# Two heads of a graph attention layer transposed by VectorE squares and SBUF transfers instead of TensorE

## The chip, the cores and the metric

The kernel runs on one core of a Trainium2 chip. The metric is the device time of one execution in microseconds. Before the change it is 3526.25 us, the median of three runs (3525.72 to 3527.4).

A core has five engines, each with its own queue of instructions in a fixed order: TensorE (PE; its weight loads are listed as PEld), VectorE (DVE), ScalarE (ACT), GpSimd (POOL) and SyncE (SP). All transfers of this kernel are issued from SP's queue; 16 DMA engines carry them out. TensorE reads SBUF and writes PSUM, which has eight banks here; VectorE or ScalarE brings a result from PSUM to SBUF (an eviction).

## The reference

`x` is 32 graphs of 512 nodes with 256 channels, in float32; `adj` is one 512 x 512 matrix for all. Four graph layers follow each other, each with its input added and a layer norm:

```python
x = _layernorm(x + _L0_gnn_ref(x, adj, ...))   # a: attention, 1 head
x = _layernorm(x + _L1_gnn_ref(x, adj, ...))   # b: transformer block, 8 heads of 32
x = _layernorm(x + _L2_gnn_ref(x, adj, ...))   # c: attention, 4 heads of 64
x = _layernorm(x + _L3_gnn_ref(x, adj, ...))   # d: bilinear attention
```

The third layer is the one whose transposes change:

```python
q = (h @ W).reshape(B, N, H, D)                       # H = 4 heads, D = 64
e = e_src[:, :, None, :] + e_dst[:, None, :, :]       # from two vectors a_src, a_dst
e = jnp.where(e >= 0, e, ALPHA * e)
e = jnp.where(mask, e, NEG_INF)
attn = jax.nn.softmax(e, axis=2)
h_prime = jnp.einsum('bijh,bjhd->bihd', attn, q)      # then elu
```

In each layer and head a graph has a 512 x 512 matrix of weights, exponentiated by rows. TensorE sums over the partitions, so to multiply this matrix with the values it has to be turned first. That is done square by square (128 x 128).

## The kernel before, in words

A graph's 512 nodes are four row blocks of 128 (`NB` = 4), handled in two halves (`F` = 2) of two blocks. A score tile `t` is one row block of one head, 128 x 512, in SBUF.

For a head of the first or third layer (class `Gat`), `attend` does this: TensorE spreads the row of destination scores over all partitions (`dst`, L755); VectorE adds the mask and takes the row maxima (`masked`, L637); ScalarE makes the bias, applies the leaky slope (L666) and the exponential with row sums (L672), in `leaky_softmax`; TensorE turns the four squares of each tile (`turn`, L549) into a PSUM bank; ScalarE or VectorE evicts that into `pT` (L492 or L494, in `copied`); and TensorE multiplies with the values (`weighted`, L561, for the third layer, two heads together; `rows_weighted`, L807, for the first and fourth). The third layer does heads 0 and 1, then heads 2 and 3. The second layer's scores are L853, its reduction L867, its exponentials L874; the fourth layer's scores are L975.

`finish` of each layer adds the input on POOL (`added`, L629), takes statistics on VectorE with a power on POOL (L603 to L609) and normalises (`normed`, L617) into the next layer's `x`. The last layer normalises into one more `x` tile, and SP stores that (L1041). SP also loads `xT` and `x` of each graph (`load`, L340); both are asked for ahead of the graph's first product.

The order of the work is not written by hand. Every step is an `op` with the engines that may do it and a duration in us that the kernel's author wrote beside it, what it reads and writes, and which pool's buffers it takes (`BUFS`: 18 tiles `t`, 8 halves `pT`, 6 `x`, and so on). `Plan.order` plays these steps through when the kernel is built: whenever an engine is free in this play, it takes the ready step with the best key. The key is made of the graph's number times `AGE`, the length of the work behind the step, and `URGENT` for the engine and stage (a letter for the layer, and 0 to 4 for projection, scores, finish, transposes, weighted product). On TensorE, `SWITCH_WEIGHT` adds a price for changing between full-array, row-tiled and column-tiled products. Up to four graphs (`WINDOW`) are in work at once. The result is one fixed order for each engine and one fixed choice of buffers and of the evicting engine; on the chip each engine goes through its order and waits where data or a buffer is not ready.

Of the kernel before, what the change touches and what calls it, by code (L numbers as in the profile page):

```python
# [14 lines left out]
ALU = mybir.AluOpType  # L15
# [12 lines left out]
BUFS = dict(t=18, pT=8, x=6, xT=3, v=5, qk=4, y=5, e=2, n=2, nT=2, hT=2, oT=4, small=8)  # L28
# [11 lines left out]
AGE = {"PE": 51, "ACT": 138, "DVE": -107, "POOL": 461, "SP": 20}  # L40
URGENT = {
    "PE": {"a0": -417, "a1": 491, "a2": -867, "b0": -448, "b1": 197, "b2": 839, "c0": -557, "c1": -258, "c2": 203, "d0": -909, "d1": -511, "d2": -1186, "a3": 1287, "a4": 1218, "b3": -47, "b4": 169, "c3": 2234, "c4": 712},
    "ACT": {"a0": -671, "a1": 422, "a2": 770, "b0": 459, "b1": 253, "b2": 93, "c0": 729, "c1": 136, "c2": -360, "d0": 573, "d1": -523, "d2": -1234, "a3": 806, "a4": -162, "b3": 370, "b4": 340, "c3": 698, "c4": -390},
    "DVE": {"a0": -247, "a1": 1195, "a2": 496, "b0": 1368, "b1": 273, "b2": -132, "c0": -1160, "c1": 19, "c2": 666, "d0": -845, "d1": -1056, "d2": -1458, "a3": 1297, "a4": 438, "b3": -527, "b4": 175, "c3": 138, "c4": 1482},
    "POOL": {"a0": -896, "a1": -817, "a2": 582, "b0": 3, "b1": -713, "b2": 227, "c0": -148, "c1": -607, "c2": 1624, "d0": 582, "d1": 1022, "d2": -1512, "a3": -446, "a4": 431, "b3": 270, "b4": 1342, "c3": 708, "c4": 734},
    "SP": {},
# [6 lines left out]
SWITCH_WEIGHT = 661  # L53
# [45 lines left out]
class Plan:  # L99
# [7 lines left out]
    def op(self, where, issue, writes=(), reads=(), takes=(), lag=0.0, port=False, form="full"):  # L107
# [10 lines left out]
        for buf in takes:  # L118
            if not buf.users and buf.tag is not None:
                o.takes.append(buf)  # L120
                self.bufs.append(buf)
                buf.users.append(o)
# [15 lines left out]
        o.after.discard(o)  # L138

# [153 lines left out]
def gnn_stack(  # L293
# [43 lines left out]
    def load(dst, out_ap, in_ap, cell=None, kb=256):  # L337
        def issue(e):
            with nc.allow_non_contiguous_dma(reason="vectors of 256 values by channel"):
                nc.sync.dma_start(out=out_ap(), in_=in_ap)  # L340

        op({SP: 0.1 + kb * 0.003}, issue, [dst if cell is None else (dst, cell)], [], lag=2.0)
# [136 lines left out]


# [62 lines left out]
    def turn(t, pT, i, name):  # L543

        ps = bank([P, NB, P], name)

        def issue(e):
            for j in range(NB):
                nc.tensor.transpose(ps[:, j], t[:, block(j)], ident)  # L549

        op({PE: 0.44}, issue, [ps], [t], [pT])
        copied(N, lambda: pT[:, :, block(i)], lambda: ps[:], [(pT, i)], [ps])

    def weighted(pv, oT, pTs, v, lo, D, us):

        def issue(e):
            for j in range(NB):
                for h, pT in enumerate(pTs):  # L560
                    nc.tensor.matmul(  # L561
                        pv[h * D : (h + 1) * D], lhsT=v[:, j, lo + h * D : lo + (h + 1) * D],
                        rhs=pT[:, j], start=(j == 0), stop=(j == NB - 1), skip_group_check=True,
                    )

        op({PE: us}, issue, [pv], [v] + pTs, [oT], form="columns")
# [13 lines left out]
    def scaled(dst, cell, lo, ps, inv, D):  # L580


        def issue(e):
# [5 lines left out]
                inv[:].unsqueeze(3).to_broadcast([P, FB, n // D, D]),  # L589
# [22 lines left out]
    def normed(y, dst, cell, lo, name):  # L612
# [8 lines left out]
        op({DVE: 0.66}, issue, [(dst, cell)], [y, mv, rstd], port=True)  # L621
# [11 lines left out]
    def masked(s, t, top, at, i):  # L633


        def issue(e):
            nc.vector.tensor_tensor_reduce(  # L637
                out=t[:], in0=s[:], in1=neg[:, i], scale=1.0, scalar=LOWEST, op0=ALU.add,
                op1=ALU.max, accum_out=top[(slice(None),) + at],
            )  # L640

        op({DVE: 0.61}, issue, [t, top], [s, (neg, i)])

    def leaky_softmax(ts, top, v, src, H, f, name):
# [3 lines left out]
        bias = tiny("bias", [P, FB, H], f"{name}_bias")  # L648
        total = tiny("total", [P, FB, H], f"{name}_total")
        inv = tiny("inv", [P, FB, H], f"{name}_inv")  # L650
        if src is not None:
            op(
                {DVE: 0.1},
                lambda e: nc.vector.tensor_tensor(top[:], top[:], v[:, part(f), src : src + H], ALU.add),
                [top], [(v, 2 * f), (v, 2 * f + 1)],
            )

        def negated(e):
            nc.scalar.activation(bias[:], top[:], AF.Prelu, alpha=SLOPE)
            nc.scalar.mul(bias[:], bias[:], -1.0)  # L660

        op({ACT: 0.3}, negated, [bias], [top])
        for (h, i), t in ts.items():

            def leaky(e, h=h, i=i, t=t):
                nc.scalar.activation(  # L666
                    t[:], t[:], AF.Prelu, alpha=SLOPE,
                    bias=0.0 if src is None else v[:, f * FB + i, src + h : src + h + 1],
                )

            def exp(e, h=h, i=i, t=t):
                nc.scalar.activation(  # L672
                    t[:], t[:], AF.Exp, bias=bias[:, i, h : h + 1], accum_out=total[:, i, h : h + 1]
                )

            op({ACT: 0.53 if src is None else 0.62}, leaky, [t], [] if src is None else [(v, f * FB + i)])
            op({ACT: 0.71}, exp, [t, total], [bias])
        pTs = []
        for h in range(H):
            pT = buf("pT", [P, NB, FN], f"{name}_pT{h}", FB)  # L680
            for i in range(FB):
                turn(ts[h, i], pT, i, f"{name}_tr{h}{i}")
            pTs.append(pT)
        op({DVE: 0.1}, lambda e: nc.vector.reciprocal(inv[:], total[:]), [inv], [total])
        return pTs, inv
# [30 lines left out]
    class Gat(Layer):  # L716
# [5 lines left out]

        def prepare(self, f):
# [17 lines left out]
        def attend(self):  # L741
            H, D, name, v = self.H, C // self.H, self.name, self.v
            G = min(H, P // D) if H > 1 else 1
            for g in range(0, H, G):
                ts = {}
                for h in range(G):
                    dst = bank([P, N], f"{name}_dst{g}{h}")
                    for i in range(NB):
                        ts[h, i] = buf("t", [P, N], f"{name}_t{g}{h}{i}")
# [7 lines left out]
                    op({PE: 0.44}, issue, [dst], [v], [ts[h, i] for i in range(NB)])  # L757
                    if h == 0:
                        tops = [
                            tiny("top", [P, FB, G], f"{name}_top{g}{f}") for f in range(F)  # L760
                        ]
                    for i in range(NB):
                        masked(dst, ts[h, i], tops[i // FB], (i % FB, slice(h, h + 1)), i)
                for f in range(F):
                    plan.stage = name[0] + "3"
                    pTs, inv = leaky_softmax(
                        {(h, i): ts[h, f * FB + i] for h in range(G) for i in range(FB)},
                        tops[f], v, C + g, G, f, f"{name}_{g}_{f}",
                    )
                    y = self.part_y(f)  # L770
                    plan.stage = name[0] + "4"
                    if H > 1:
                        pv = bank([P, FN], f"{name}_pv{g}{f}")
                        oT = buf("oT", [P, 1, FN], f"{name}_oT{g}{f}")
                        weighted(pv, oT, pTs, v, g * D, D, 1.86)
                        copied(FN, lambda oT=oT: oT[:, 0], lambda pv=pv: pv[:], [oT], [pv])
                        ps = turned_back(oT, 1, y, f"{name}_{g}{f}")
                        op({DVE: 0.4}, scaled(y, 0, g * D, ps, inv, D), [y], [ps, inv])
                    else:
                        pv = bank([P, FB, C], f"{name}_pv{f}")  # L780
                        rows_weighted(pv, pTs[0], v, y)
                        op({DVE: 0.62}, scaled(y, 0, 0, pv, inv, C), [y], [pv, inv])
# [18 lines left out]
    def rows_weighted(pv, pT, v, y):  # L801

        for i in range(FB):

            def issue(e, i=i):
                for j in range(NB):
                    nc.tensor.matmul(  # L807
                        pv[:, i], lhsT=pT[:, j, block(i)], rhs=v[:, j, 0:C],
# [3 lines left out]
            op({PE: 1.73}, issue, [pv], [(pT, i), v], [y])  # L812

    class Transformer(Layer):
# [14 lines left out]
        def attend(self):  # L829
            name, q_sb, k_sb = self.name, self.q, self.k  # L830
            for f in range(F):
# [4 lines left out]
                for c in range(NC):  # L836
                    ts = {}
                    for i in range(FB):
                        all_s = {}
                        for q0 in range(0, Q, S_HEADS):  # L840
                            heads = range(q0, q0 + S_HEADS)
                            ss = {
                                q: bank([P, N], f"{name}_s{f}{c}{i}{q}") for q in heads
                            }
                            for q in heads:
                                ts[q, i] = buf("t", [P, N], f"{name}_t{f}{i}{c}{q}")

                            all_s.update(ss)

                            def scores(e, i=i, ss=ss, c=c, f=f):  # L850
                                for q, s in ss.items():
                                    at = slice(q * D1, (q + 1) * D1)
                                    nc.tensor.matmul(  # L853
                                        s[:], lhsT=q_sb[at, c, block(f * FB + i)], rhs=k_sb[at, c],
                                        start=True, stop=True,
                                    )

                            op(
                                {PE: 0.95}, scores, list(ss.values()), [(q_sb, f), k_sb],
                                [ts[q, i] for q in heads], form="rows",  # L860
# [233 lines left out]
```

## Time and profile before

| | |
|---|---|
| median of three runs | 3526.25 us |
| profiled execution | 3525.66 us |
| its span, first to last instruction | 3523.9 us |
| granted TensorE clock | 0.999 |
| TensorE busy | 3501.5 us (99%) |
| VectorE busy | 2973.8 us (84%) |
| ScalarE busy | 2807.6 us (80%) |
| GpSimd busy | 869.1 us (25%) |
| transfers' share of the 16 DMA engines | 4.9% |
| transposes of score tiles (L549) | 7168 squares |
| SP queue waiting for the last layer's rows (L1041) | 3349.8 us |

A group line of the profile reads: line, engine, operation, written tile <- read tiles, shape, count | busy us, mean ns of one | idle us of the engine just before, and who ended it. A group's busy time is the union of its intervals; matmuls are pipelined, so one instruction's interval (274 ns) overlaps the next, and the tail of a group overlaps the group behind it. A timeline line has start, duration, engine, line, instruction and how many of them in a row. The chain of work that ended last is followed back from the last instruction to what released each step. Issue lines give count, size and the median time from issue to landing.

### The profile page before, as it was taken

To read this page: it belongs to the slowest core of one execution; us is meant where nothing else is said; L and a number is where in the kernel's file an instruction comes from. 1 tells how busy PE (TensorE), PEld (TensorE's weight loads), DVE (VectorE), ACT (ScalarE), POOL (GpSimd) and SP (SyncE) were. 2 spreads that over 40 slices of the span, in tenths; PEclk is the share of its full clock that TensorE was granted. 3 is DMA by queue.
4 is the path that set the end of the run, shared out by engine and by line. 5 is a ranking of instruction groups with operands and counts; after the bars stand their busy time and mean duration, and the time that the engine had idled before them with its cause. 6 is when DMAs were issued, how large, how long until landed. Compare 5 with 4: busy or idle time off the path is not lost.

```text
span 3523.9 us, 68878 instructions
## 1 busy us (share of the span) xinstructions
PE 3501.5 (99%) x24728; PEld 2685.4 (76%) x24728; DVE 2973.8 (84%) x8792; ACT 2807.6 (80%) x6856; POOL 869.1 (25%) x840
## 2 busy tenths in 40 slices
PE   8999999999999999999999999999999999999999
PEld 7777777778777787877878778687787877878777
DVE  7789888888888888888888888888888888888886
ACT  6798877878788787887888878887788877888786
POOL 1222222222222222222222222222222222222322
PEclk9999999999999999999999999999999999999999
DMA  3000100001000010000100001000010000100000
GB/s 95 7 2 1 37 1 19 19 1 37 1 19 19 1 37 1 19 19 1 37 1 19 19 1 37 1 19 19 1 37 1 19 19 1 37 1 19 19 7 19
DMA packets 56918, 59.41 MB, mean 17 GB/s; under 512 B 3968, under 2 KB 55808, under 8 KB 56576
## 3 DMA queue, kind: packets, MB, share of 16 engines
q1 hardware_dynamic: 56576, 55.00, 4.9%
q8 instruction: 196, 3.21, 0.4%
q14 instruction: 146, 1.20, 0.1%
HBM read 38.21 MB, written 16.78 MB: 16 GB/s over the span
## 4 chain that ended last, share of the span: by engine, by line
PE 99%; DVE 1%; ACT 0%; DMA 0%; issue 0%; SPq 0%; POOLq 0%; POOL 0%; DVEq 0%
PE ps L549 23%; PE ps L561 13%; PE ps L520 13%; PE ps L807 12%; PE ps L535 10%; PE ps L853 8%; PE ps L733 7%; PE ps L975 6%; PE ps L505 3%; PE ps L755 2%; PE ps L575 2%; DMA xT<-in_x_T 0%; SPq L340 0%; DVE st L603 0%; DVE rstd L606 0%
## 5 line engine op out<-in xcount | busy, mean ns | idle before, releaser
L549 PEld LDWEIGHTS ps<-ident,t 128*128 128x128 f32 x7168 | 805.5, 141 | 178.4 <-issue 38.7
L549 PE MATMUL ps<-ident,t 128*128 128x128 f32 x7168 | 898.4, 274 | 1.0 <-ACT t L874 0.8
L874 ACT ACTIVATE t<-t,low 128x512 f32<-128x512 f32 x1024 | 734.8, 735 | 41.5 <-DVE low L867 41.5
L492 ACT COPY pT<-ps 128x512 f32<-128x512 f32 x1099 | 594.1, 593 | 119.9 <-PE ps L549 116.4
L867 DVE CUSTOM_DVE_ANT_0 t<-ps,neg 128x512 f32<-128x512 f32 x1024 | 649.0, 686 | 46.2 <-PE ps L853 43.6
L629 POOL TENSOR_TENSOR y<-y,x 128x512 f32<-128x512 f32 x256 | 330.0, 1290 | 1371.7 <-DVE y L586 493.3
L609 POOL TENSOR_TENSOR rstd<-rstd,mhalf 128x2 f32<-128x2 f32 x384 | 297.2, 774 | 1049.1 <-DVE rstd L606 934.3
L637 DVE CUSTOM_DVE_ANT_0 t<-ps,neg 128x512 f32<-128x512 f32 x768 | 492.3, 683 | 69.9 <-PE ps L975 59.4
L672 ACT ACTIVATE t<-t,bias 128x512 f32<-128x512 f32 x768 | 544.0, 709 | 0.4
L561 PE MATMUL ps<-pT,v 128*32 128x256 f32 (+1 forms) x6144 | 486.1, 382 | 0.0
L494 DVE COPY pT<-ps 128x512 f32<-128x512 f32 x693 | 451.3, 682 | 40.1 <-PE ps L549 37.8
L807 PE MATMUL ps<-v,pT 128*128 128x256 f32 x2048 | 465.5, 379 | 0.0
L666 ACT ACTIVATE t<-t,v 128x512 f32<-128x512 f32 x640 | 418.4, 715 | 32.5 <-DVE top L637 32.4
L561 PEld LDWEIGHTS ps<-pT,v 128*32 128x32 f32 (+1 forms) x6144 | 260.4, 118 | 208.1 <-issue 22.6
L807 PEld LDWEIGHTS ps<-v,pT 128*128 128x128 f32 x2048 | 378.5, 190 | 48.2 <-issue 2.3
L853 PE MATMUL ps<-qk,qk 32*128 32x512 f32 x2048 | 291.7, 639 | 0.0
L603 DVE BATCH_NORM_STATS2 st<-y 128x6 f32<-128x256 f32 x768 | 285.2, 413 | 4.5 <-POOL y L629 3.1
L975 PE MATMUL ps<-xT,qk 128*128 128x512 f32 x512 | 241.7, 596 | 0.0
L520 PE MATMUL ps<-xT,w_qkv_sb 128*128 128x256 f32 x1024 | 230.8, 379 | 0.0
L617 DVE TENSOR_SCALAR x<-y,mv,rstd 128x256 f32<-128x256 f32 x512 | 219.3, 474 | 3.7 <-POOL rstd L609 1.9
L874 ACT ACTIVATION_READ_ACCUMULATOR t<-t,low 128x1 f32 x1024 | 214.3, 209 | 0.0
L586 DVE TENSOR_TENSOR y<-ps,inv 128x512 f32<-128x512 f32 (+1 forms) x256 | 140.9, 551 | 83.9 <-PE ps L807 72.0
(84 smaller groups left out, 4630.4 us busy)
## 6 DMA issues: line engine op xcount, KB each, us to landing
xT<-in_x_T SPq DMA_DIRECT2D x64, 256.0 KB, 3.2
x<-in_x SPq DMA_DIRECT2D x32, 512.0 KB, 4.5
out<-x SPq DMA_DIRECT2D x64, 256.0 KB, 2.2
t<-in_adj SPq DMA_DIRECT2D x4, 256.0 KB, 6.8
w_qkv_sb<-in_L_gnn_w_qkv SPq DMA_DIRECT2D x1, 768.0 KB, 7.2
w_sb<-in_L_gnn_w SPq DMA_DIRECT2D x2, 256.0 KB, 5.8
t<-in_L_gnn_W SPq DMA_DIRECT2D x2, 256.0 KB, 2.8
w_sb<-in_L_gnn_W SPq DMA_DIRECT2D x1, 256.0 KB, 2.8
```

The lines of the kernel that those rows point to most:

```text
L492: nc.scalar.copy(dst(), ps())
L494: nc.vector.tensor_copy(dst(), ps())
L520: nc.tensor.matmul(ps[:, c], lhsT=w[:, k, lo + c * P : lo + (c + 1) * P], rhs=xT[:, k, nlo : nlo + FN], start=(k == 0), stop=(k == NC - 1),)
L549: nc.tensor.transpose(ps[:, j], t[:, block(j)], ident)
L561: nc.tensor.matmul(pv[h * D : (h + 1) * D], lhsT=v[:, j, lo + h * D : lo + (h + 1) * D], rhs=pT[:, j], start=(j == 0), stop=(j == NB - 1), ...
L637: nc.vector.tensor_tensor_reduce(out=t[:], in0=s[:], in1=neg[:, i], scale=1.0, scalar=LOWEST, op0=ALU.add, op1=ALU.max, accum_out=top[(sli ...
L672: nc.scalar.activation(t[:], t[:], AF.Exp, bias=bias[:, i, h : h + 1], accum_out=total[:, i, h : h + 1])
L807: nc.tensor.matmul(pv[:, i], lhsT=pT[:, j, block(i)], rhs=v[:, j, 0:C], start=(j == 0), stop=(j == NB - 1),)
L853: nc.tensor.matmul(s[:], lhsT=q_sb[at, c, block(f * FB + i)], rhs=k_sb[at, c], start=True, stop=True,)
L867: nc.vector.tensor_tensor_reduce(out=t[:], in0=s[:], in1=neg[:, f * FB + i], scale=-1.0 / math.sqrt(D1), scalar=HIGHEST, op0=ALU.add, op1= ...
L874: nc.scalar.activation(t[:], t[:], AF.Exp, bias=low[:, i, h : h + 1], scale=-1.0, accum_out=total[:, i, h : h + 1],)
L975: nc.tensor.matmul(s[:], lhsT=hh[:, k, block(f * FB + i)], rhs=xT[:, k], start=(k == 0), stop=(k == NC - 1),)
```

## The change

In heads 2 and 3 of the third layer, in 30 of the 32 graphs (all but the last two, `PLAIN`), the transposes on TensorE and their evictions are replaced. VectorE transposes each tile in place in squares of 32 x 32 (the flip). Sixteen transfers per head then move the squares to where a full transpose puts them: transfer (a, b) takes from partitions 32a to 32a+31 the 32 columns at 32b of each of the 16 squares of 128, and writes them to partitions 32b on at columns 32a. Such a head's four tiles lie in one buffer of a pool of their own, `tq`, with two buffers.

The third and first layer now run by head rather than by half: one `leaky_softmax` over four row blocks, one buffer `pq` for the turned matrix of a whole head (five of them, in place of eight halves `pT`), with each row block's squares side by side. The weighted product of the third layer so reads its moving operand in two runs of 128. The second layer puts two heads into one `pq`.

`x` of a graph is asked for after the first layer's score row on TensorE (`later`), not ahead of the graph. The last layer normalises in place in `y` and stores from there. The pools change (`t` 18 to 15, `x` 6 to 5, `nT` 2 to 3), as do all weights of the plan's keys, and the space kept for GpSimd's own transfers, which the kernel doesn't use, becomes 1024.

```diff
-BUFS = dict(t=18, pT=8, x=6, xT=3, v=5, qk=4, y=5, e=2, n=2, nT=2, hT=2, oT=4, small=8)
+BUFS = dict(t=15, x=5, xT=3, v=5, qk=4, y=5, e=2, n=2, nT=3, hT=2, oT=4, tq=2, pq=5, small=8)
...
-SWITCH_WEIGHT = 661
+SWITCH_WEIGHT = 172
+SQ = 32
+DMA_US = 0.63
+FLIP_US = 0.66
+BY_TRANSFERS = {"a": (), "b": (), "c": (2, 3), "d": ()}
+PLAIN = 2
...
+    def turned(ts, pT, blocks, by_transfers, name):
+        if not by_transfers:
+            for i in blocks:
+                turn(
+                    ts[i], pT, i, lambda i=i: pT[:, i * NB : (i + 1) * NB], f"{name}_tr{i}"
+                )
+            return
+        for i in blocks:
+            op({DVE: FLIP_US}, lambda e, t=ts[i]: nc.vector.transpose(t(), t()), [ts[i].use], [])
+        t = ts[0].buf
+        def squares():
+            return t[:].rearrange("p i (j n) -> p (i j) n", n=P)
+        for a in range(P // SQ):
+            def move(e, a=a):
+                here = slice(a * SQ, (a + 1) * SQ)
+                for b in range(P // SQ):
+                    there = slice(b * SQ, (b + 1) * SQ)
+                    nc.sync.dma_start(out=pT[there, :, here], in_=squares()[here, :, there])
+            op({SP: P // SQ * DMA_US}, move, [(pT, a)], [t], lag=2.0)
...
+        def fetch(self, later):
+            x, b = self.x, int(self.name[1:])
+            load(
+                x, lambda: x[:], self.source[b].rearrange("(k p) c -> p k c", p=P), kb=512, later=later
+            )
...
                 for h in range(G):
...
+                    by_transfers = (
+                        g + h in BY_TRANSFERS[name[0]] and int(name[1:]) < B - PLAIN
+                    )
+                    ts = rows(NB, f"{name}_t{g}{h}", by_transfers)
+                    pT = buf("pq", [P, NB * NB, P], f"{name}_pT{g}{h}", NB)
...
+                    o = op({PE: 0.44}, issue, [dst], [v], [t.buf for t in ts])
+                    if H == 1:
+                        self.fetch(o)
                     for i in range(NB):
-                        masked(dst, ts[h, i], tops[i // FB], (i % FB, slice(h, h + 1)), i)
+                        masked(dst, ts[i], top, i)
+                    plan.stage = name[0] + "3"
+                    leaky_softmax(ts, top, v, C + g + h, total, h, range(NB), f"{name}_{g}{h}")
+                    turned(ts, pT, range(NB), by_transfers, f"{name}_{g}{h}")
+                    pTs.append(pT)
...
-            normed(y, dst, f, f * FB, f"{self.name}_n{f}")
+            normed(y, y, None, 0, f"{self.name}_n{f}")
+            def store(e):
+                nc.sync.dma_start(
+                    out=out[int(self.name[1:])].rearrange("(k p) c -> p k c", p=P)[:, part(f)], in_=y[:]
+                )
+            op({SP: 0.45}, store, [], [y], lag=2.0)
...
-    nc = bacc.Bacc("TRN2", target_bir_lowering=False, num_devices=1)
+    nc = bacc.Bacc("TRN2", target_bir_lowering=False, num_devices=1, dynamic_dma_scratch_size=1024)
```

## The prediction

> **What bounds the kernel now.** I read the engines' busy shares first, then the chain of work that ended last, then the groups of instructions.
>
> ```profile
> span 3523.9 us, 68878 instructions
> PE 3501.5 (99%) x24728; PEld 2685.4 (76%) x24728; DVE 2973.8 (84%) x8792; ACT 2807.6 (80%) x6856; POOL 869.1 (25%) x840
> ...
> PE 99%; DVE 1%; ACT 0%; DMA 0%; issue 0%; SPq 0%; POOLq 0%; POOL 0%; DVEq 0%
> ...
> L549 PE MATMUL ps<-ident,t 128*128 128x128 f32 x7168 | 898.4, 274 | 1.0 <-ACT t L874 0.8
> ...
> L492 ACT COPY pT<-ps 128x512 f32<-128x512 f32 x1099 | 594.1, 593 | 119.9 <-PE ps L549 116.4
> ...
> L494 DVE COPY pT<-ps 128x512 f32<-128x512 f32 x693 | 451.3, 682 | 40.1 <-PE ps L549 37.8
> ```
>
> TensorE is busy for 3501.5 of 3523.9 us and is the whole chain. The other 22.4 us are 12.0 at the start (waiting for the first xT), 8.2 after its last product, and 2 of gaps. VectorE and ScalarE have 550 and 716 us to spare. So TensorE work removed comes off the time, provided that TensorE still never waits. The largest TensorE group is the transposes of the exponentiated scores (L549); their evictions (L492, L494) lie on engines with room.
>
> The group's 898.4 us count the overlapping tail of each run, so the price is taken from start to start, in the timeline of TensorE, and for the other two engines in theirs:
>
> ```profile
> 3453.02 1.52 PE L549 MATMUL ps<-ident,t 128*128 128x128 f32 x12
> 3454.38 0.60 PE L755 MATMUL ps<-ident,v 128*128 128x128 f32 x4
> 3454.82 1.91 PE L549 MATMUL ps<-ident,t 128*128 128x128 f32 x16
> 3456.56 0.60 PE L755 MATMUL ps<-ident,v 128*128 128x128 f32 x4
> ```
>
> Columns: start, duration, instruction. 1.36 us for 12 and 1.74 for 16 are 113 and 109 ns each. Over five stretches of 120 us, 1188 of these transposes took 112.5 ns each. The same way, 128x512 takes VectorE 0.61 us, an exponential 0.71 us on ScalarE, an eviction there 0.51.
>
> **The change, part by part.**
>
> *Transposes removed.* The new order holds 6208 of them instead of 7168: 8 row blocks x 4 squares in 30 of 32 graphs = 960. 960 x 112.5 ns = **-108.0 us** on TensorE, all on the path.
>
> *Evictions removed, flips added.* 240 evictions go and 240 VectorE square transposes of 128x512 come. With the redistributed remainder VectorE has 406 evictions of this kind instead of 693, ScalarE 1146 instead of 1099. VectorE: -287 x 0.61 + 240 x 0.61 = -29 us; ScalarE +47 x 0.51 = +24. No row shows the flip. I take the nearest, any 128x512 VectorE operation at 0.61; [...]from above twice, 1.2, which makes VectorE +115. Even so VectorE stays below 3100 of 3400 us: hidden under TensorE. Were that cover gone, all 240 x 0.61 = 146 us would count.
>
> *Moves added, and the wait they make.* Each of the 60 heads takes 16 transfers on SP's queue, each 32 partitions x 16 runs of 128 bytes (64 KB, 512 packets, 32 per DMA engine). That is 960 transfers on a queue that had 184. Their landing is what the weighted product of heads 2 and 3 now waits for, and behind it all of TensorE's fixed order. What this trace shows of transfers:
>
> ```profile
> 1517.26 0.95 SPq L340 DMA_DIRECT2D xT<-in_x_T  x2
> 1518.31 0.42 SPq L340 DMA_DIRECT2D x<-in_x  x1
> ...
> xT<-in_x_T SPq DMA_DIRECT2D x64, 256.0 KB, 3.2
> ...
> out<-x SPq DMA_DIRECT2D x64, 256.0 KB, 2.2
> ```
>
> An issue takes 0.42 to 0.48 us and does not grow with the packet count (x has 512 packets, xT 256). A store landed after 2.2 us. In the packet records, one of 4 bytes took 8.9 ns, of 256 bytes 18.2, of 1 KB 51: so 128 bytes about 13.5 ns, and 32 of them 0.43 us, less than an issue. From below, then, 0.48 us each. From above, a packet of 128 bytes costs what 1 KB costs here at best (46 ns): 1.47 us each. The kernel's own plan counts 0.63.
>
> How much room there is I get from the order. I add up TensorE's instructions at start-to-start durations (this gives 3494 us for the kernel before, against 3501.5 busy; 3386 after; 105.5 us per graph in the middle, where each graph repeats the same pattern). Call 0 the end of the four score products of the second layer that VectorE reduces just ahead of head 3's last two masked blocks. The first weighted product of heads 2 and 3 stands at **+23.4 us**. In between, step by step:
> - VectorE, started at -0.7, does 4 reductions and 2 masked blocks, 6 x 0.61: +3.0.
> - ScalarE: last leaky pass 0.62, two small bias operations 0.35, one foreign exponential 0.71, four exponentials 4 x 0.71: +7.5.
> - Last flip: +8.2.
> - 16 moves at 0.48 or 0.63, and 2.2 to land: +18.1 or +20.5.
>
> So the data are there 3 to 5 us early. No stall as long as a move takes under (23.4 - 8.2 - 2.2)/16 = **0.81 us**. Head 2 has some 73 us between its flips and that product and never decides.
>
> [...] I follow the rows: the flip has already ordered the inside of each square, so the runs are 128 bytes, and packets of 4 to 256 bytes took 9 to 18 ns here. [...]
>
> *SP's queue.* Behind head 3's moves stand, in order, two output stores, two loads of a later graph's xT, and x. The stores wait for the last layer's normalised rows, on VectorE at about +24, after the moves are issued (+15.9 to +18.3), so the moves delay nobody. The xT loads leave at about +25, land 3.2 later at +28.5, and TensorE first reads them at +30.3. Storing from y only drops the copy to another tile; the normalisation (408 ns a row) stays. x is asked for after the first layer's score row, behind xT, and first needed by POOL, after that layer's weighted products: 0. If these moves took over 1 us each, the xT loads would be late next.
>
> *Form switches, start.* With other weights in the order, changes from full-array work to scores or weighted products go from 396 to 416, and back likewise. A group of four transposes took 0.53 us ahead of such a change against 0.44 elsewhere, and about 0.05 more after it: 20 x 0.14 = **+3 us**. At the start x no longer holds up weights, but the adjacency comes later: 0, plus or minus 3. The small bias, top and reciprocal operations fall by some 190, off the path.
>
> *Buffers.* 18 score tiles become 15 (two heads have tiles of their own), x 6 becomes 5. VectorE's summed work never gains on TensorE's by more than about 3 us within a graph. I count 0; each 1% of TensorE idle would be 34 us.
>
> *The third layer's moving operand* is now two runs of 128 instead of one of 256: no row; 0 taken, 10 ns on 2048 products would be 20 us.
>
> Sum: 3523.9 - 108.0 + 3 = 3418.9 span; +1.8 around it in the profiled execution (3525.66), and the median of the runs lies 0.6 above that: **3421 us**.
>
> **Rivals.**
> - *Moves too slow for the room: slower than before.* Decides from (23.4 - 8.2 - 2.2 + 3.5)/16 = 1.03 us a move, since 105/30 = 3.5 us of stall per graph eat the gain. With 46 ns packets, 1.47 us: 16 x 1.47 + 2.2 = 25.7, 10.5 us late, x 30 = +315: 3736. For it: nothing in this trace moves such short runs within SBUF. Against: the packet records. 0.15.
> - *Moves between 0.81 and 1.03 us.* Some of the gain is given back[...]. 0.15.
> - *TensorE waits elsewhere*: a dearer flip (at 1.2 us the four no longer keep up with the exponentials, the last ends 2 us later, and VectorE is at 90%), fewer tiles, the operand in two runs. One per cent: 3455. Against: VectorE at 86%, ScalarE at 83%. 0.11.
> - *Nothing changes*: the transposes are gone from the order, so only a stall of just 3.5 us per graph gives this. 0.03.
>
> **How the numbers follow.** A measurement of this kernel tells about 0.2% (7 us). The sum as it stands: 0.56, 3408 to 3434 (start, switches, gaps). With the partial cases the range 3406 to 3500 holds about 0.8. Faster is 0.56 + 0.15 + 0.11 = 0.82, the same 0.03, slower 0.15.
>
> **What would show it.** Right: 6208 transposes; TensorE still 99% of the chain, busy near 3395 us; no wait of the weighted product for a transfer; a move landing in 2 to 3 us. Wrong: in the chain a DMA into pq ahead of the third layer's weighted products, some 30 waits of equal length; SP's queue issuing at 1 us a move; xT loads waited for; or many short waits for ps, t or pq.

## The result and the profile after

The changed kernel takes **3486.84 us** (median of four runs, 3485.2 to 3488.76). The kernel before, on the same chip, takes 3526.44 (four runs). The ratio is 0.9888 (95% interval 0.9871 to 0.9905): faster by 39.6 us. The direction was predicted, but the predicted gain was 105 us. Some 66 us of it are missing: the profiled span is 3484.6 us where the sum gave 3418.9. The range 3406 to 3500 holds the time only because it was widened for the partial cases; the sum as it stood, 3408 to 3434, does not.

The page of the changed kernel, the same rows as were shown of before, with the new transfers:

```profile
span 3484.6 us, 67428 instructions
PE 3448.1 (99%) x23768; PEld 2606.2 (75%) x23768; DVE 2930.5 (84%) x8605; ACT 2810.0 (81%) x6851; POOL 852.2 (24%) x840
...
PE 97%; DVE 1%; ACT 1%; SPq 1%; issue 0%; DMA 0%; POOLq 0%; POOL 0%; DVEq 0%
...
L529 ACT COPY pq<-ps 128x512 f32<-128x512 f32 x1146 | 620.5, 586 | 295.4 <-PE ps L586 292.9
L586 PE MATMUL ps<-ident,t 128*128 128x128 f32 x6208 | 834.8, 276 | 6.3 <-ACT t L743 6.3
...
L531 DVE COPY pq<-ps 128x512 f32<-128x512 f32 x406 | 272.9, 681 | 41.1 <-PE ps L586 36.2
...
pq<-tq SPq DMA_DIRECT2D x960, 64.0 KB, 2.1
xT<-in_x_T SPq DMA_DIRECT2D x64, 256.0 KB, 3.6
...
out<-y SPq DMA_DIRECT2D x64, 256.0 KB, 2.2
```

Line numbers have moved: L586 was L549, L529 and L531 were L492 and L494. The 960 transposes and the evictions are gone as counted, a move lands in 2.1 us, and TensorE is still busy for 99%. But it is busy for 3448 us, not for 3395. The page alone does not say why, because it models the ends of matmuls: a short wait of TensorE is filled by the modelled tail of the matmul before it, and counts as busy.

So I added up every matmul's time from its start to the next matmul's start, by kind of work. TensorE's score-tile transposes went from 7168 at 112.5 ns (806.1 us) to 6208 at 116.2 (721.1): 108.0 us less by count, and 23.0 more because each takes longer. The second layer's scores (L853 before, L927 after), whose number is the same, went from 134 to 148 ns: 29.0 us more. The turns of x (L542) took 11.1 more. Each other kind changes by less than 8 us, some up and some down. With each kind at its undisturbed price the work fell by some 106 us (an estimate from these sums), so the sum of -108 and +3 held. What came back is waiting.

In the steady middle a graph takes 107.49 us, where it took 109.19 before; the order at start-to-start durations gives 105.5. Each repeated graph has three waits of TensorE. This is the changed kernel's timeline at the first two, TensorE, VectorE and GpSimd only (start, duration, engine, line, instruction, how many in a row; brackets hold an engine's idle time and what ended it):

```profile
1076.84 1.14 PE L927 MATMUL ps<-qk,qk 32*128 32x512 f32 x8
...
1080.18 0.29 DVE L650 BATCH_NORM_AGGREGATE mv<-st 128x2 f32<-128x6 f32 x2
1080.41 1.27 POOL L1003 TENSOR_TENSOR x<-x,c_sb 128x512 f32<-128x512 f32 x1
1080.50 1.20 DVE L651 TENSOR_TENSOR rstd<-mv,eps 128x2 f32<-128x2 f32 x1
...
1081.63 0.68 DVE L941 CUSTOM_DVE_ANT_0 t<-ps,neg 128x512 f32<-128x512 f32 x1
...
1081.85 2.25 PE L927 MATMUL ps<-qk,qk 32*128 32x512 f32 x8
...
1082.37 0.30 PEld L927 LDWEIGHTS ps<-qk,qk 32*128 32x128 f32 x4 [0.22 <-DVE low L941]
...
1084.03 1.73 PE L586 MATMUL ps<-ident,t 128*128 128x128 f32 x12
...
1084.79 0.16 DVE L651 TENSOR_TENSOR rstd<-mv,eps 128x2 f32<-128x2 f32 x1
```

A group of eight score products takes 1.14 us at 1076.84 and 2.25 us at 1081.85: the second one waits in its middle, by 1.05 us in the median graph, for a PSUM bank that a reduction of VectorE (L941) frees. The reduction starts late, because the instruction ahead of it on VectorE, L651, takes 1.20 us. L651 adds the layer norm's epsilon to 128 x 2 numbers and elsewhere takes 0.16 us (the last line). While it hangs, GpSimd runs L1003, which adds a layer-norm constant (the second layer's last bias) to 128 x 512 of x. The whole trace bears this out: of the 384 instructions of L651, 68 take longer than 0.2 us. Each of these 68 starts while a GpSimd addition on 128 x 512 runs (30 times L1003, 37 times L674) or multiplication (once L999), and ends 15 to 23 ns after it. The other 316 start while GpSimd runs nothing. Of the 30 behind L1003, 29 take over 1 us, one in each of 29 graphs.

The L586 group right behind is longer too: 1.64 us from its start to the next group's, where twelve take 1.31 at their shortest. That is the second wait, 0.33 us, for exponentials that come late in their turn.

The third wait, of 0.46 us, has nothing to do with VectorE. In the same kernel's timeline, TensorE finishes turning the third layer's x, ScalarE evicts it, and only then can the projection start:

```profile
1058.64 1.09 PE L542 MATMUL ps<-ident,x 128*128 128x128 f32 x8
...
1059.34 1.07 ACT L529 COPY xT<-ps 128x512 f32<-128x512 f32 x2 [1.02 <-PE ps L542]
...
1059.97 2.05 PE L804 MATMUL ps<-wg_sb,xT 128*128 128x264 f32 x8 [0.24 <-ACT xT L529]
```

From 1058.64 to 1059.97 are 1.33 us for eight transposes that need some 0.9 (8 x 112.5 ns), and the new order puts nothing between the two.

### The profile page after: what moved, and what is told of

It is laid out like the page before. It is cut to its first block, busy times and chain, and to the rows that moved or that the text cites. A ratio compares the mean times of both kernels' runs of the same rounds, so it can differ in the third digit from the quotient of the medians.

```text
span 3484.6 us, 67428 instructions
## 1 busy us (share of the span) xinstructions
PE 3448.1 (99%) x23768; PEld 2606.2 (75%) x23768; DVE 2930.5 (84%) x8605; ACT 2810.0 (81%) x6851; POOL 852.2 (24%) x840
## 4 chain that ended last, share of the span: by engine, by line
PE 97%; DVE 1%; ACT 1%; SPq 1%; issue 0%; DMA 0%; POOLq 0%; POOL 0%; DVEq 0%
PE ps L586 20%; PE ps L603 13%; PE ps L889 13%; PE ps L557 13%; PE ps L572 9%; PE ps L927 9%; PE ps L804 7%; PE ps L1065 6%; PE ps L542 3%; PE ps L833 2%; PE ps L617 2%; SPq L712 1%; ACT xT L529 0%; DVE t L941 0%; ACT t L737 0%
## 5 line engine op out<-in xcount | busy, mean ns | idle before, releaser
L586 PEld LDWEIGHTS ps<-ident,t 128*128 128x128 f32 x6208 | 703.8, 141 | 233.8 <-ACT pq L529 44.8
L529 ACT COPY pq<-ps 128x512 f32<-128x512 f32 x1146 | 620.5, 586 | 295.4 <-PE ps L586 292.9
L586 PE MATMUL ps<-ident,t 128*128 128x128 f32 x6208 | 834.8, 276 | 6.3 <-ACT t L743 6.3
L941 DVE CUSTOM_DVE_ANT_0 t<-ps,neg 128x512 f32<-128x512 f32 x1024 | 655.0, 684 | 25.5 <-ACT e L874 10.0
L674 POOL TENSOR_TENSOR y<-y,x 128x512 f32<-128x512 f32 x256 | 329.3, 1286 | 1237.6 <-DVE y L1087 620.5
L603 PE MATMUL ps<-pq,v 128*32 128x256 f32 (+1 forms) x6144 | 485.2, 382 | 2.4 <-issue 2.4
L889 PE MATMUL ps<-v,pq 128*128 128x256 f32 x2048 | 457.6, 381 | 0.2 <-ACT pq L529 0.2
L889 PEld LDWEIGHTS ps<-v,pq 128*128 128x128 f32 x2048 | 383.4, 190 | 62.3 <-issue 11.5
L603 PEld LDWEIGHTS ps<-pq,v 128*32 128x32 f32 (+1 forms) x6144 | 263.3, 119 | 217.2 <-issue 42.2
L743 ACT ACTIVATE t<-t,bias 128x512 f32<-128x512 f32 x528 | 374.5, 710 | 1.1
L682 DVE CUSTOM_DVE_ANT_0 t<-ps,neg 128x512 f32<-128x512 f32 x528 | 342.3, 685 | 32.2 <-PE ps L1065 19.6
L927 PE MATMUL ps<-qk,qk 32*128 32x512 f32 x2048 | 320.9, 639 | 0.0
L531 DVE COPY pq<-ps 128x512 f32<-128x512 f32 x406 | 272.9, 681 | 41.1 <-PE ps L586 36.2
L737 ACT ACTIVATE t<-t,v 128x512 f32<-128x512 f32 x400 | 270.1, 718 | 11.2 <-DVE top L682 11.1
L557 PEld LDWEIGHTS ps<-xT,w_qkv_sb 128*128 128x128 f32 x1024 | 189.4, 190 | 23.4 <-issue 0.4
```

Of the source, the lines that this page charges most:

```text
L529: nc.scalar.copy(dst(), ps())
L557: nc.tensor.matmul(ps[:, c], lhsT=w[:, k, lo + c * P : lo + (c + 1) * P], rhs=xT[:, k, nlo : nlo + FN], start=(k == 0), stop=(k == NC - 1),)
L586: nc.tensor.transpose(ps[:, j], t()[:, block(j)], ident)
L603: nc.tensor.matmul(at, lhsT=v[:, j, lo + h * D : lo + (h + 1) * D], rhs=p, start=(j == 0), stop=(j == NB - 1), skip_group_check=True,)
L674: lambda e: nc.gpsimd.tensor_add(y[:], y[:], x[:, part(f)]),
L682: nc.vector.tensor_tensor_reduce(out=t(), in0=s[:], in1=neg[:, i], scale=1.0, scalar=LOWEST, op0=ALU.add, op1=ALU.max, accum_out=top[:, i ...
```

## The experiments

All experiments on the changed kernel but the last two keep its order on every engine. The first theory was: TensorE waits because L651 is held up while an instruction of GpSimd runs, 1.20 us instead of 0.16. The expectations call it the port theory; what the runs show is the wait, not what in the chip causes it. The prediction's rivals stood against it: the moves slow the engines (the transfer theory), the flips are too dear, the tiles and pools are too few (the buffer theory).

### The addition of epsilon left out

```diff
-nc.vector.tensor_tensor(rstd[:], mv[:, :, 1], eps, ALU.add)
...
-... nc.gpsimd.tensor_tensor(rstd[:], rstd[:], mhalf, ALU.pow), [rstd], [])
+... nc.gpsimd.tensor_tensor(rstd[:], mv[:, :, 1], mhalf, ALU.pow), [rstd], [mv])
```

> The changed kernel, the same order on every engine; VectorE no longer adds the 1e-5 to the variance (L651, 128x2), GpSimd raises the variance itself to the power. It leaves out the epsilon of the layer norms. Port theory (VectorE's small addition waits while GpSimd works on SBUF; 1.20 us instead of 0.16 just ahead of the reductions that TensorE waits for, in every graph): TensorE's waits of 1.05 and 0.33 us per graph go, the one of 0.46 stays, 29 x 1.3 = -38: about 3449. Buffer theory (15 score tiles and the new pools are too few) and transfer theory (960 moves slow the engines): 3487, plus or minus 4.

Measured: 3449.07 us (3448.56 to 3450.89), ratio to the kernel before 0.9781 (0.9767 to 0.9796). The span falls by 37.5 us, to 3447.1, and a graph in the middle takes 106.19. The same place in this kernel's timeline:

```profile
1071.94 0.29 DVE L650 BATCH_NORM_AGGREGATE mv<-st 128x2 f32<-128x6 f32 x2
1072.15 0.66 DVE L940 CUSTOM_DVE_ANT_0 t<-ps,neg 128x512 f32<-128x512 f32 x1
1072.18 1.28 POOL L1002 TENSOR_TENSOR x<-x,c_sb 128x512 f32<-128x512 f32 x1
...
1073.90 1.14 PE L926 MATMUL ps<-qk,qk 32*128 32x512 f32 x8
...
1074.97 1.53 PE L586 MATMUL ps<-ident,t 128*128 128x128 f32 x12
```

GpSimd's addition runs as before (1.28 us), now beside a reduction (0.66 us), and neither is held up. The score group is back to 1.14 us. Of the wait behind it, in the L586 group, 0.2 us go (1.42 us to the next group instead of 1.64), not all 0.33. An instruction that works on two numbers per partition, 0.16 us when undisturbed, cost 37.5 us of the span.

### GpSimd's addition left out

```diff
-lambda e: nc.gpsimd.tensor_add(x[:, part(f)], x[:, part(f)], over_rows(c2_sb[:])),
+lambda e: None,
```

> The changed kernel, the same order; GpSimd's addition of the second layer's last bias to x (L1003, 1.27 us) does nothing, so that bias is left out. Port theory: L651 takes 0.16 us at that place too, although VectorE's instructions are all there, and the wait of 1.05 us goes in each graph: about 3455. If it is VectorE's amount of work that is too large there: 3487.

Measured, in one run: 3456.88 us, span 3455.1, 106.43 us a graph. VectorE keeps its L651, and its group line in this kernel reads

```profile
L651 DVE TENSOR_TENSOR rstd<-mv,eps 128x2 f32<-128x2 f32 x384 | 73.6, 192 | 13.3
```

against

```profile
L651 DVE TENSOR_TENSOR rstd<-mv,eps 128x2 f32<-128x2 f32 x384 | 103.8, 270 | 13.3
```

in the changed kernel, and against 188 ns in the kernel before (shown below). The wait of 1.05 us is gone. So it takes both instructions, VectorE's and GpSimd's, at the same time: removing either one gives most of the same gain (29.5 us of span here, 37.5 without L651). The 0.2 us in the L586 group do not go here (1.57 us to the next group), although every L651 near it takes 0.16. So they are not the hold-up; they fit the plain 0.16 us that the addition takes on VectorE, and in 29 graphs they are 6 of the 8 us between the two runs.

### GpSimd's addition done twice

```diff
-lambda e: nc.gpsimd.tensor_add(x[:, part(f)], x[:, part(f)], over_rows(c2_sb[:])),
+lambda e: [nc.gpsimd.tensor_add(x[:, part(f)], x[:, part(f)], over_rows(c2_sb[:])) for _ in range(2)],
```

> The changed kernel, the same order; GpSimd adds the second layer's last bias twice (L1003, two instructions of 1.27 us), so the result holds that bias once too often. Port theory: VectorE's small addition then waits for both, about 1.27 us longer, and TensorE's wait at that place grows from 1.05 to about 2.3 us in each of some 29 graphs: 3487 + 37 = about 3524. Buffer and transfer theories: GpSimd is busy 25% of the time and nothing waits for that x for long: 3487.

Measured, in one run: 3488.28 us, within the changed kernel's own spread (3485.2 to 3488.76). The theory that the wait grows with GpSimd's work expected 3524 and missed. The timeline of this kernel shows why:

```profile
1083.07 2.62 POOL L1004 TENSOR_TENSOR x<-x,c_sb 128x512 f32<-128x512 f32 x2
1083.17 1.19 DVE L651 TENSOR_TENSOR rstd<-mv,eps 128x2 f32<-128x2 f32 x1
1084.28 0.68 DVE L941 CUSTOM_DVE_ANT_0 t<-ps,neg 128x512 f32<-128x512 f32 x1
```

Two GpSimd additions run for 2.62 us, but L651 still takes 1.19: it ends at 1084.36, about when the first of the two does (1084.34, an estimate from the 1.27 us that one takes in the changed kernel). Over all 384 its mean is 276 ns, against 270 in the changed kernel. The theory has to be narrowed: L651 waited for one GpSimd instruction, the one that ran when it started, and not for the one queued behind it: some 1.0 us (1.19 less 0.16).

### One input instead of two

```diff
-nc.vector.tensor_tensor(rstd[:], mv[:, :, 1], eps, ALU.add)
+nc.vector.tensor_scalar(rstd[:], mv[:, :, 1], EPS, None, ALU.add)
```

> The changed kernel, the same order; VectorE still adds the epsilon, as many instructions, but as a tensor-scalar operation with a constant (one input in SBUF) instead of a tensor-tensor operation with two. [...] as without the addition, about 3450. [...] (the normalisation, also tensor-scalar, took 0.85 us longer beside GpSimd): 3487.

Measured: 3486.9 us (3485.19 to 3487.21), ratio 0.9887 (0.9874 to 0.9901): the higher of the two expectations, nothing gained. The group line of this kernel:

```profile
L651 DVE TENSOR_SCALAR rstd<-mv 128x2 f32<-128x2 f32 x384 | 106.9, 278 | 13.3
```

278 ns in the mean: with a constant in place of the second tile the instruction waits as before, again 68 times, 30 of them for over 1 us. So a second tile as input is not what the wait depends on (278 ns with one, 270 with two). What it does depend on, these runs do not show.

### Epsilon added by GpSimd: nothing left out

```diff
-nc.vector.tensor_tensor(rstd[:], mv[:, :, 1], eps, ALU.add)
...
+def power(e):
+    nc.gpsimd.tensor_tensor(rstd[:], mv[:, :, 1], eps, ALU.add)
+    nc.gpsimd.tensor_tensor(rstd[:], rstd[:], mhalf, ALU.pow)
+op({POOL: 0.7}, power, [rstd], [mv])
```

> The changed kernel, the same order; the epsilon is added by GpSimd, as an instruction of its own ahead of the power, and VectorE's L651 is gone. Nothing is left out. Port theory: as without the epsilon, 3449, if GpSimd's extra 0.5 to 0.7 us per layer norm is not waited for; up to 3460 where it is. Buffer and transfer theories: 3487.

Measured: **3450.18 us** (3449.45 to 3450.91), ratio 0.9783 (0.9767 to 0.9799). The sum is where the power already is, on an engine that idles for three quarters of the span. It costs GpSimd 384 instructions of 0.22 us and gives back 36.7 us. This is the fastest complete version of the study: 76 us below the kernel before, 37 below the changed kernel.

### The same edit on the kernel before

The edit is that of the first experiment (epsilon left out), on the kernel before the change.

> The kernel before, its own order, with the same edit (the epsilon left out, no addition on VectorE). Port theory: in the kernel before that addition took 188 ns on average and stood ahead of nothing that TensorE waited for: 3526, plus or minus 4. If taking 384 instructions from VectorE helps any such kernel: some 40 us less here too, 3486.

Measured: 3524.12 us (3523.24 to 3525.22), ratio 0.9992 (0.9984 to 1.0001). That is 2.8 us less, and the interval just includes no change: the addition costs at most some 6 us there, not 37. The kernel before has the same two instructions, and its group line for this addition reads

```profile
L606 DVE TENSOR_TENSOR rstd<-mv,eps 128x2 f32<-128x2 f32 x384 | 72.2, 188 | 13.3
```

In its trace 33 of the 384 are held up, only 2 of them to over 1 us, so its order places the two side by side less often and for less long. The cost belongs to the new order, which puts them side by side in 29 of the 32 graphs, ahead of a reduction that TensorE is about to need.

### The flips left out

```diff
-op({DVE: FLIP_US}, lambda e, t=ts[i]: nc.vector.transpose(t(), t()), [ts[i].use], [])
+op({DVE: FLIP_US}, lambda e: None, [ts[i].use], [])
```

> The changed kernel, the same order; the 240 square transposes on VectorE are left out, the moves stay. The weights of heads 2 and 3 are turned wrongly. Port theory: the flips end some 30 us before the reductions that are late, so the waits stay: 3480 to 3488. If the flips' 160 us of VectorE time cause the waits, they go: about 3430.

Measured, in one run: 3483.29 us, 3.6 below the changed kernel's median and 1.9 below its fastest run. All three waits stay (1.05, 0.33 and 0.46 us). Its waits view (who <- for what: us in total, times, longest) has the late reductions and the eviction of xT as in the changed kernel, where they are 52.0 and 7.0 us:

```profile
ACT t L948 <- DVE low L941: 52.1, 67, 1.6
...
PE ps L804 <- ACT xT L529: 7.0, 29, 0.3
```

So 240 instructions, without which VectorE is busy for 2794.7 us instead of 2930.5, are hidden, and a dearer flip is not the cause of the miss.

### Four more issues of moves per head

The last four of a head's sixteen moves go as two halves each.

```diff
+halves = (slice(0, 8), slice(8, 16)) if a == 3 else (slice(0, 16),)
+for k in halves:
-    nc.sync.dma_start(out=pT[there, :, here], in_=squares()[here, :, there])
+    nc.sync.dma_start(out=pT[there, k, here], in_=squares()[here, k, there])
```

> The changed kernel, the same order; the last four of a head's sixteen moves are made as two halves each, twenty issues per head, the same bytes. By the prediction's chain (data 3 to 5 us early) 4 x 0.63 = 2.5 us more is not seen: 3487. By the changed kernel's trace (last move landed about 0.7 us before the weighted product) it comes 1.8 us late in each graph, 30 x 1.8 = +54: about 3540.

Measured: 3518.36 us (3514.79 to 3520.56), ratio 0.9977 (0.9967 to 0.9986), 108.49 us a graph. That lies between the two expectations. Four more issues are at least 4 x 0.627 = 2.5 us; 1.0 us of it reached TensorE in each graph. So the room left is about 1.5 us: the changed kernel does not wait for its moves, but nearly. The 0.7 us of the expectation was read in one graph, and a tight one; the median of the 30 graphs in the same trace is 1.4. The waits view of this kernel shows twelve waits that the changed kernel, apart from one of 2.4 us, has not:

```profile
PE ps L603 <- DMA pq<-tq: 14.9, 12, 6.7
PEld ps L603 <- DMA pq<-tq: 5.8, 4, 1.8
```

These are only part of the 30.9 us by which the span grew; the short waits again hide in the modelled ends.

### Half the eviction of the third layer's xT

The eviction ahead of the third layer's projection copies half of its columns; the other half of xT stays as it was. The product still reads all of it.

```diff
+half = FN // 2 if name[0] == "c" else FN
-N, lambda: dst[:, :, dlo : dlo + FN], lambda: ps[:].rearrange("p k i n -> p k (i n)"),
+N, lambda: dst[:, :, dlo : dlo + half],
+lambda: ps[:].rearrange("p k i n -> p k (i n)")[:, :, 0:half],
```

> The changed kernel, the same order; of each turned x of the third layer only half the columns are brought from PSUM to SBUF (256 instead of 512), so half of that layer's xT is stale. If the second wait (0.46 us, first projection of the third layer behind the eviction of xT, with nothing in TensorE's order in between) is the length of that eviction, it falls by some 0.22 us in each of about 29 graphs: -6, 3481. If TensorE waits there for something else: 3487.

Measured: 3481.64 us (3480.47 to 3481.79), ratio 0.9872 (0.9856 to 0.9889), 5.2 us less than the changed kernel. In the steady middle the step from the last turn to the projection is the only one of TensorE's that changes, by 0.21 us a graph. In this kernel's timeline the projection follows the turn of x after 1.11 us instead of 1.33:

```profile
1058.37 1.09 PE L542 MATMUL ps<-ident,x 128*128 128x128 f32 x8
...
1059.48 2.05 PE L806 MATMUL ps<-wg_sb,xT 128*128 128x264 f32 x8
```

So this wait is the length of an eviction that stands in the path without cover.

### Without transfers, the rest of the change kept

```diff
-PLAIN = 2
+PLAIN = 32
```

> The changed kernel without its transfers: all heads in all 32 graphs turned by TensorE, the rest of the change (pools, plan weights, x late, stores from y) kept; the order is the plan's new one for that. By the prediction's sum the rest is worth +3: about 3530. If the rest of the change brings TensorE waits by itself: 3550 to 3600.

Measured, in one run: 3737.42 us. Both expectations missed, by 137 us and more. With other work in the plan, the plan's keys give another order on every engine, and it is a bad one: this kernel's chain reads

```profile
PE 79%; ACT 12%; DVE 7%; issue 1%; DMA 0%; SPq 0%; POOL 0%; POOLq 0%; DVEq 0%; ACTq 0%
```

A fifth of it lies on other engines. The run tells nothing of the change's other parts (processing by head, the late x, the store from y): they can't be priced with an order made for something else. What they are worth alone stays open.

### Other weights for the plan

On top of epsilon added by GpSimd, another set of the plan's weights, and so another order.

```diff
-SWITCH_WEIGHT = 172
+SWITCH_WEIGHT = 654
...
```

`AGE` and `URGENT` change as well.

> The kernel with the epsilon on GpSimd and other weights of the plan's keys, so a new order on every engine; the work is the same. If the prediction's sum was right but for waits that the order brings, an order with fewer waits comes near the sum, 3421: expected 3425 to 3445. If something in the transfers themselves holds TensorE at 3450: 3450 or more, in any order.

Measured: 3549.21 us (3546.48 to 3551.86), ratio 1.0064 (1.005 to 1.0078): slower than both kernels, where a gain was expected. Stretches of this kernel (window, its length, then busy us and instructions of PE, PEld, DVE, ACT, POOL; clock, share of the DMA engines, GB/s):

```profile
0.00:360.00 360.00, 330.06 (x2272) 249.84 (x2273) 276.82 (x785) 259.90 (x627) 82.30 (x114) 0.98 0.16 40
...
1420.00:3400.00 1980.00, 1975.47 (x13793) 1498.93 (x13790) 1634.02 (x4747) 1636.15 (x4012) 536.36 (x705) 1.00 0.17 36
```

and the first stretch of the kernel that it was made from:

```profile
0.00:360.00 360.00, 345.65 (x2482) 263.57 (x2483) 290.37 (x829) 283.25 (x683) 89.84 (x123) 1.00 0.17 42
```

From 1420 us on TensorE is full. The loss is in the first 1400 us, where TensorE stands still for 2 to 7 us at a time. Why that order starts so badly stays open. Behind that start a graph takes 106.19 us, exactly as in the kernel that it was made from. In the middle this order is no faster, so the run does not tell whether one with fewer waits would come nearer to the sum.

## Why the prediction was right and wrong

**Transposes removed: right.** 6208 remain, and at undisturbed prices TensorE's work fell by some 106 us, where -108 and +3 for the form switches were predicted.

**Evictions removed, flips added: right.** A flip took 0.60 us from start to start (0.61 taken), and leaving all of them out moved the time by 3.6 us. They are hidden under TensorE, as stated.

**Moves added: right that there is no stall, wrong on the room.** The changed kernel's answer for the tile `tq` (counts, and ns min/median/max of one):

```profile
L712 SPq DMA_DIRECT2D pq<-tq x960: 585/627/2114, 196.1 to 3319.6; - x192
...
L700 DVE STREAM_TRANSPOSE tq<-tq x240: 667/670/715, 193.0 to 3307.9; 128x512 f32<-128x512 f32 x120
...
  PE ps L603: 2.4, 1
```

The median issue is 0.627 us, within the 0.48 to 0.63 taken, and the weighted product (L603) waited for a move once in the whole kernel, for 2.4 us. A packet of 128 bytes took 12.0 ns in the packet records (13.5 taken). The rival with packets as dear as those of 1 KB (46 ns, 1.47 us a move) did not come true. But the timeline of a middle graph shows how near it was:

```profile
1026.31 36.07 SPq L712 DMA_DIRECT2D pq<-tq  x32
...
1048.51 2.48 DVE L700 STREAM_TRANSPOSE tq<-tq 128x512 f32<-128x512 f32 x4
...
1064.61 3.67 PE L603 MATMUL ps<-pq,v 128*64 128x256 f32 x32
1064.89 1.03 SPq L1101 DMA_DIRECT2D out<-y  x2
```

The prediction's zero point, the end of the score products, is at 1041.16 here. The weighted product came at +23.4 exactly as added up, but the last flip ended at 1050.99, +9.8 instead of +8.2. Most of this is the chain's first term: VectorE began the four reductions at 1041.58, +0.4 instead of -0.7. The moves behind the flip ran until 1062.38, which is 0.71 us each from one to the next (11.4 / 16), and the last had landed by 1063.8, 0.8 us early. This is a tight graph. Over the 30 graphs the median is 0.67 us a move and 1.4 us early; 28 graphs lie between 0.5 and 1.5, in one the last move lands just as the product starts, and in the first it is 2.8 us late, which is the one wait above. The run with four more issues gives 1.5. So the room was 1.4 us, not the 3 to 5 predicted. With the flip at +9.8, the prediction's own formula for the limit gives (23.4 - 9.8 - 2.2)/16 = 0.71 us a move instead of 0.81, against 0.67 measured. The forecast was right here with little to spare.

**SP's queue: right.** The stores left at 1064.89 (+23.7), after the moves, and not later.

**The moving operand in two runs: right.** The third layer's weighted products went from 113.8 to 114.7 ns each: 1.9 us in all.

**Buffers, the step that failed.** It said: "VectorE's summed work never gains on TensorE's by more than about 3 us within a graph. I count 0". So TensorE's waits were put at nothing on the strength of a sum over VectorE's durations, and the span came out 65.7 us longer than the prediction's sum. I priced each VectorE instruction at what it took in the trace of before, as if that were its own. In the new order a 0.16 us addition meets a GpSimd instruction and takes 1.20, just where VectorE has no slack towards TensorE. The code of the kernel before held a hint of it: its plan marks the normalisation with `port=True` (L621) and in its play does not start it while GpSimd works (L204), but the step that holds the epsilon addition has no such mark. A second part of the waits is not VectorE's at all: the eviction that no TensorE work covers, below.

Of the three rivals that end later than the forecast, "TensorE waits elsewhere" is what happened, at twice its estimated size (66 us, not 34) and for none of the three reasons given for it: the dearer flip and the operand in two runs are shown not to cost, fewer tiles were not tried by themselves, though the largest wait went without any change to them, and what did cost was not named. The "many short waits for ps, t or pq" under what would show it wrong are what the trace has.

The missing 65.7 us of span, added up:

- VectorE's epsilon addition: 37.5 us, shown by the run without it. 29.5 of them are the hold-up by GpSimd's L1003, shown by the run without that; some 6 fit the plain 0.16 us that the addition takes on VectorE.
- The eviction of the third layer's xT without cover: 0.46 us in some 29 graphs, 13 us; the half eviction took 5.2 of them, the rest was not tried. This is work that stood in the order and that a sum over TensorE alone can't see.
- The first head's moves: TensorE waits 2.4 to 2.8 us, once, at 218 us.
- The last two graphs, which use no transfers: one wait of 5.5 to 5.8 us for an exponential, shown in the changed kernel's timeline as

```profile
3411.57 1.11 PE L586 MATMUL ps<-ident,t 128*128 128x128 f32 x4 [5.54 <-ACT t L743]
```

- The start is 1.8 us earlier than before (first product at 10.13, not 11.97), which the prediction left at 0.
- That leaves some 8 us, which would be waits of 0.1 to 0.3 us a graph, not followed further.

## What to carry to other kernels

When one engine is the bound at 99%, do not read "busy" as "never waits": take start-to-start sums by kind of work, before and after, and the kind whose price rose is where the wait sits. A duration from a trace belongs to its neighbours as well as to the instruction (0.16 or 1.20 us for the same L651); when an order changes, look for small VectorE instructions that now run beside GpSimd and ahead of something the bounding engine needs, and put them on GpSimd itself, which here gave 36.7 us. A margin worked out from a chain of medians (here 3 to 5 us) should be measured before it is called safe (it was 1.4), and in every graph rather than in one; four extra transfer issues are a cheap way.

## What the runs showed of the hardware that was not expected

- L651, a VectorE addition of 128 x 2 elements with its inputs in SBUF, was held for the rest of a running GpSimd addition of 128 x 512: 1.20 us instead of 0.16. In the changed kernel it was held 68 times (once by a multiplication), and each time it ended 15 to 23 ns after GpSimd's instruction. With two such additions in a row it still waited for one only (1.19). Written with a constant in place of the second tile it waited as well (278 ns in the mean, against 192 with GpSimd's addition away).
- A VectorE normalisation of 128 x 256 beside a GpSimd addition was stretched too: two L662 beside L674 took 1.69 us together instead of 0.73, and L674 took 1.37 instead of 1.27. This was seen in the changed kernel's timeline and not tried by itself.
- A reduction (L941, 128 x 512, with an input in PSUM) was not held by the same GpSimd addition: 0.66 us beside it in the run without epsilon, and in the changed kernel 0.69 at most in 36 that overlap an L1003; its mean there is 0.68.
- Transfers inside SBUF in runs of 128 bytes, 64 KB each, went out every 0.67 us in the median from one queue and landed after 2.1 us (2.0 to 4.2). A packet of 128 bytes took 12.0 ns in the mean, where one of 1 KB took 52.
